# A quarter of a shared expert issued inside the stage before it, and a new plan of every engine's order

## The chip, the cores and the metric

The kernel runs on one core of one Trainium2 chip. The metric is the device time of one execution in microseconds; smaller is better. Of the kernel before there are three timed runs and one execution taken by the hardware profiler.

## The reference

The input is x, 2048 tokens of 128 channels, in float32. Four layers follow one another, each with a mixing part and a feed-forward part, and each part ends with `x = layernorm(x + part(x))` or the like. For this change two parts of the third layer matter, a chunked attention part and a mixture of experts with one shared expert that all tokens pass:

```
# L2 attention: 8 sequences of 256 tokens, each on its own
x = la attention, lf feed-forward, sa attention, pf feed-forward (each with its norm)
x = layernorm(x + ...)

# L2 experts ("moe2"): E=8, K=2, capacity 320 rows each
xn = xf * rsqrt(mean(xf*xf) + eps);   logits = xn @ router_w.T
topk_p, topk_i = top_k(softmax(logits), 2);  rw = topk_p / sum(topk_p)
dispatch = for each expert the first 320 tokens that chose it
eout = (silu(xg @ rg) * (xg @ ru)) @ rd            # per expert, 320 x 128, inner size 512
routed = eout, weighted, added back to the rows they came from
shared = silu(x @ sg) * (x @ su) @ sd              # all 2048 tokens, inner size 1024
x = layernorm(x + shared + routed)
```

After it comes the fourth layer: an attention with decay ("typed" here), again over 8 sequences of 256 tokens, and a ternary linear layer.

## The kernel before

The kernel runs six stages in a row: `rglru`, `local_mamba`, `moe1`, `chunked`, `moe2`, `typed`. Channels lie on the 128 partitions, tokens along the free axis, all in SBUF between stages.

**Who sets the order.** The Python code records instructions stage by stage. Then the class `_Order` takes all of them with their dependences and plans, engine by engine, in which order they are issued. It simulates the engines with a table of lengths per form of instruction (`LENGTHS`: busy time and latency in nanoseconds), ranks instructions by the place where the code recorded them plus a correction by engine, tile and stage (`BIAS`), and prefers to stay with what an engine is set to (`STAY`: a rank bonus for the same shape of TensorE tile, and for the same activation table on ACT). A table change is charged `TABLE` = 1283 ns. `impose` fixes the order found. So a change at one place, or a new number in these tables, moves instructions everywhere.

**Activation tables.** ACT must hold the table set of the function that it runs. Exp and Ln share one set (group 1 in `SETS`), Silu, Gelu and Sigmoid have their own. In the kernel before, the code itself places loads of the Exp/Ln set by hand (`exp_ln`, which calls `keep`), at places that the order then has to respect; one more hand-placed load fetches the Silu set early in the first routing (`if t0:`). All other loads are put in by the compiler just ahead of the activation that needs them.

**The chunked stage.** `on_pe` interleaves the eight sequences in three streams; `one_sequence(b)` goes through attention `la`, feed-forward `lf`, attention `sa`, feed-forward `pf`, a norm, `logits`, and `route2`. The stage's PSUM banks are K (3), A (2), B (1) and M (2). `route2` ranks two experts per token on VectorE (small instructions), with Exp/Ln on ACT for the row scale (`four`), counts ranks with a product on TensorE (`cum`), and scatters rows into the buffer `places` on POOL, four indirect DMAs (L1623) per sequence. Sequence 7 needs the counts of sequence 6 (`sum2`). By the time the last sequence runs out there are few streams left to fill TensorE; this is called the tail here.

**The moe2 stage** has banks A (2), B (2), M (3) and S (1). The shared expert is done in four quarters of 512 tokens, each a generator `shared(i)` with eight steps ("blocks"): `pg` and `pu` (128x512 products), Silu on ACT (L2052), a multiply on VectorE (L2057, tile `sh`) and four products into `acc`. Order in the code: two steps of `shared(0)`, the rest of the last routing, `rows_of` (five transfers `got<-places`, of which the second and fourth are issued on ACT's queue, L1643), the other steps of `shared(0)`, the eight experts (`bt` transposes, `pg`, `pu`, `py`, rows written to `ybuf`), then `shared(1)` to `shared(3)`, with 32 indirect gathers from `ybuf` on POOL (L1658) beside them: four at once, then one for each step, held by a wait for the Silu of that step:

```python
            for _ in shared(1):
                next(fetch)
            self.x = y
            first = chain(results(0, self.ty), self.typed_before(0))
            for i in (2, 3):
                for _ in shared(i):
                    next(first, None)
                    next(fetch, None)
```

`results` multiplies the gathered rows by their gates and normalises; `typed_before` prepares a sequence of the typed attention, with rotations `q`, `k` (L2205), masked keys `km` (L2212) on POOL. The typed stage's softmax multiplies `e` (L2262) are on POOL too.

Of the kernel before, what the change touches and what calls it, by code (L numbers as in the profile page):

```python
# [311 lines left out]
class _Order:  # L312
# [14 lines left out]
    STAY = dict(PE=80, ACT=740)  # L327
    BIAS = {
        "ACT  1": 100, "ACT  5": 585, "ACT bt 3": 5, "ACT bt 5": -775, "ACT d 2": -425, "ACT da 2": -45, "ACT e 2": -5, "ACT e 4": 965, "ACT e 6": -20,
        "ACT got 3": 575, "ACT h 2": -200, "ACT ix 4": 15, "ACT k 2": 265, "ACT lavp 2": 210, "ACT lnrs 1": -10, "ACT lnrs 2": -160, "ACT lnsq 1": -135,  # L330
        "ACT lnsq 2": 15, "ACT ot 2": 10, "ACT ptsb 2": -595, "ACT ptsb 6": -515, "ACT q 2": 20, "ACT qsq 2": 10, "ACT r 2": -5, "ACT rg 1": 10,
        "ACT rg 2": -915, "ACT rn 2": 15, "ACT rs 4": 340, "ACT rs 6": -690, "ACT s 6": 200, "ACT sakq 2": -10, "ACT sg 3": -550, "ACT sh 5": -2525,
        "ACT spe 1": -220, "ACT spt 1": -50, "ACT st 6": 100, "ACT sz 2": 280, "ACT v 2": 885, "ACT vs 4": 320, "ACT xchunked 2": 15, "ACT xs 2": -610,
        "DVE biasfull 3": -335, "DVE biaspart 3": -20, "DVE bt 5": -5, "DVE c 1": 590, "DVE centre 0": 320, "DVE d 2": 10, "DVE decaypart 4": -600,
        "DVE e 4": 570, "DVE four 4": 100, "DVE fs 4": -70, "DVE gate 4": 340, "DVE get 2": 200, "DVE got 4": 530, "DVE identb 0": -50, "DVE k 6": 500,
        "DVE lg 2": 2240, "DVE lo 4": -265, "DVE mv 4": -660, "DVE mv 5": 100, "DVE mv 6": -485, "DVE nm 2": -3975, "DVE nm 6": 4960, "DVE nth 4": -45,
        "DVE oh 2": -725, "DVE oh 5": -10, "DVE ptsb 2": -3895, "DVE ptsb 6": 895, "DVE put 4": -395, "DVE put 5": 55, "DVE q 5": -825, "DVE q 6": -475,
        "DVE rc 2": -1225, "DVE rc 6": 10, "DVE route 2": -55, "DVE s 5": 10, "DVE sares 2": 70, "DVE sel 2": -1590, "DVE sg 3": -140, "DVE sm 4": 2720,
        "DVE spl 1": -215, "DVE ss 2": 370, "DVE st 4": 85, "DVE st 6": 1645, "DVE sum 4": 170, "DVE t 2": 440, "DVE u 2": 250, "DVE vs 4": 50,
        "DVE we 4": 1425, "DVE xc 2": 460, "DVE xla 4": -15, "DVE xlocal 2": -5, "DVE xmoe 5": -200, "DVE xmoe 6": -580, "DVE xpf 4": -370,  # L340
        "DVE xrglru 2": 120, "DVE xsa 4": 80, "DVE z 4": -1990, "PE a 2": -100, "PE acc 5": 155, "PE b 2": -35, "PE bt 3": 75, "PE bt 5": 50,
        "PE cum 2": -995, "PE cum 4": -25, "PE cum 5": -615, "PE fold 2": 2915, "PE g 2": -4155, "PE gate 2": 785, "PE kps 4": 135, "PE less 2": 295,
        "PE lg 2": 1680, "PE lg 4": 50, "PE ln 2": -10, "PE o 2": 10, "PE o 6": -10, "PE pg 5": 150, "PE ps 4": -15, "PE pt 4": -130, "PE pu 3": 220,
        "PE py 3": -200, "PE py 5": 170, "PE qk 2": 25, "PE qkt 2": -720, "PE raw 2": -8675, "PE rows 2": 400, "PE sc 2": -50, "PE sc 4": 65, "PE sc 6": 5,
        "PE v 5": 290, "PE vps 2": 4075, "PE vps 4": 25, "PE wo 2": 75, "PE wo 6": -85, "PE wout 2": -115, "PE xin 2": 1180, "PE xps 2": -2540, "PE y 2": 20,
        "PE z 2": -450, "PE zt 5": 560, "PE zt 6": 25, "POOL d 2": 130, "POOL e 6": -30, "POOL got 4": -200, "POOL h 2": 370, "POOL k 5": 400,
        "POOL k 6": 850, "POOL km 6": 1240, "POOL mean 0": 1510, "POOL places 5": -200, "POOL q 6": 20, "POOL rest 4": -65, "POOL rg 1": -800,
        "POOL rg 2": -200, "POOL rot 2": -400, "POOL s 6": -750, "POOL t 2": 550, "POOL zero 0": -655, "POOL zeros 1": 385, "SP bc 2": -970, "SP cst 3": 5,
        "SP got 3": 355, "SP got 5": 350, "SP rottable 0": 80, "SP rows 4": 210, "SP rowschunked 4": -105, "SP vec 0": -830, "SP w 0": 15, "SP w 3": 115,
        "SP wattn 2": 585, "SP wffn 2": 705, "SP wlocal 0": 1175, "SP wmoe 4": 520, "SP xs 2": -105, "SP ybuf 5": -200,  # L350
    }
    LENGTHS = {
        "ACT  LoadActFuncSet  ": (1178, 1283), "ACT d Ln 128x512 128x512": (535, 640), "ACT da Exp 128x255 128x255": (398, 503),
        "ACT e Abs 128x256 128x256": (460, 565), "ACT e Exp 128x128 128x128": (420, 525), "ACT e Exp 128x256 128x256": (461, 566),
        "ACT e Exp 128x512 128x512": (527, 632), "ACT four Exp 128x2 128x2": (100, 205), "ACT got DMACopy 128x512 128x512": (454, 3611),
        "ACT h TensorCopy 64x255 64x255": (295, 400), "ACT lnrs Exp 128x256 128x256": (315, 420), "ACT ot TensorCopy 128x512 128x512": (486, 591),
        "ACT qsq Square 128x512 128x512": (494, 599), "ACT r Relu 128x256 128x256": (460, 565), "ACT rg Exp 128x1020 128x1020": (1039, 1144),
        "ACT rg Exp 128x1024 128x1024": (998, 1103), "ACT rg Ln 128x1024 128x1024": (950, 1055), "ACT rn Exp 128x16 128x16": (110, 215),
        "ACT rn Ln 128x16 128x16": (112, 217), "ACT rs Exp 128x2 128x2": (96, 201), "ACT rs Ln 128x2 128x2": (98, 203),
        "ACT sh Silu 128x512 128x512": (492, 597), "ACT v TensorCopy 128x512 128x512": (485, 590), "ACT xc Identity 128x256 128x256": (460, 565),  # L360
        "ACT xc Silu 128x512 128x512": (526, 631), "ACT xchunked TensorCopy 128x256 128x256": (263, 368), "ACT xmoe Identity 128x256 128x256": (404, 509),
        "ACT xs TensorCopy 33x256 33x256": (257, 362), "ACT xsq Square 128x128 128x128": (297, 402), "DVE biaspart TensorCopy 96x256 96x256": (197, 282),
        "DVE decay TensorScalarPtr 128x512 128x512": (508, 593), "DVE decaypart TensorCopy 128x512 128x512": (331, 416),
        "DVE four TensorScalarPtr 128x4 128x4": (76, 160), "DVE ge TensorScalarPtr 128x256 128x256": (380, 465),
        "DVE ge TensorScalarPtr 85x256 85x256": (372, 457), "DVE got TensorScalarPtr 128x128 128x128": (258, 343),
        "DVE h TensorTensor 128x256 128x256": (312, 397), "DVE hs TensorScalarPtr 128x1024 128x1024": (2189, 2274),
        "DVE hs TensorTensor 128x1024 128x1024": (1116, 1201), "DVE mv BNStatsAggregate 128x2 128x6": (82, 167),
        "DVE nm TensorTensor 128x8 128x8": (66, 151), "DVE ptsb TensorCopy 128x512 128x512": (589, 674), "DVE rc Reciprocal 128x16 128x16": (160, 245),
        "DVE rc Reciprocal 128x4 128x4": (84, 169), "DVE rc Reciprocal 128x8 128x8": (106, 191), "DVE rg TensorScalarPtr 128x256 128x256": (577, 662),
        "DVE rg TensorTensor 128x1024 128x1024": (1109, 1194), "DVE rottable TensorScalarPtr 128x256 128x256": (261, 346),  # L370
        "DVE s TensorScalarPtr 128x128 128x128": (247, 332), "DVE s TensorTensor 128x256 128x256": (323, 408),
        "DVE sm TensorReduce 128x16 128x512": (593, 678), "DVE ss TensorReduce 128x8 128x512": (594, 679), "DVE st BNStats 128x6 128x128": (197, 282),
        "DVE sum TensorReduce 128x32 128x448": (810, 895), "DVE t TensorScalarPtr 128x256 128x256": (384, 469),
        "DVE t TensorTensor 128x512 128x512": (593, 678), "DVE vec TensorTensor 128x1 128x1": (59, 144), "DVE vec TensorTensor 85x1 85x1": (59, 144),
        "DVE vs TensorCopy 128x512 128x512": (594, 679), "DVE wlocal TensorScalarPtr 128x682 128x682": (481, 566),
        "DVE x TensorScalarPtr 128x256 128x256": (368, 453), "DVE xc TensorScalarPtr 128x254 128x254": (383, 468),
        "DVE xc TensorScalarPtr 128x255 128x255": (384, 469), "DVE xla TensorScalarPtr 128x256 128x256": (442, 527),
        "DVE xlocal TensorTensor 128x256 128x256": (311, 396), "DVE xpf TensorScalarPtr 128x256 128x256": (562, 647),
# [64 lines left out]
    def group(self, i):  # L443
# [5 lines left out]
        if e == "ACT":  # L449
            return 1 if op == "LoadActFuncSet" else self.SETS.get(str(x.func).split(".")[-1]) if op == "Activation" else None  # L450
        return None

    def change(self, i):
        x, e, op = self.ops[i]
        if e == "ACT":
            return 0.0 if op == "LoadActFuncSet" else self.TABLE
# [315 lines left out]
class _Kernel:  # L772
# [125 lines left out]
    def exp_ln(self, last=None):  # L898

        i = self.nc.scalar.preload_act_table_set("natural_log_exp_and_others")  # L900
        if last is not None:
            self.issue_after([i], last)
# [1508 lines left out]
```

## Time and profile before

| | before |
|---|---|
| median of 3 runs | 1642.47 us (1641.91 to 1643.14) |
| profiled execution, own time | 1644.68 us |
| its span | 1642.9 us |
| mean granted TensorE clock | 0.942 |
| PE busy | 1417.4 us, 86% |
| DVE (VectorE) busy | 1102.3 us, 67% |
| ACT (ScalarE) busy | 968.6 us, 59% |
| POOL (GpSimd) busy | 587.5 us, 36% |

"PE" is TensorE's matmul, "PEld" its weight load. The profiled execution is 2.2 us longer than the median. A line of a timeline gives the start, the duration, the engine, the source line, the operation with output and inputs, the count, and in brackets how long the engine had been idle and what released it; "issue" means that nothing in the profile held it. A line of windows gives a stretch of the span, its length, the busy time and count of each engine, the granted clock (1.00 is full speed), the DMA share and GB/s. Shares over the whole span are averages over stages with different limits. By the tiles in the trace `rglru`, `local_mamba` and `moe1` take up to about 862 us, `chunked` with its tail up to about 1288 us, `moe2` up to about 1442 us, and `typed` the rest.

### The profile page before, as it was taken

How to read it: one execution, taken by the hardware profiler on the slowest of the kernel's cores; microseconds unless marked ns; L12 is line 12 of the kernel's file. 1: busy time of each engine (PE TensorE's matmuls, PEld its weight loads, DVE VectorE, ACT ScalarE, POOL GpSimd, SP SyncE). 2: the span in 40 equal slices, each digit the busy share in tenths (PEclk: the TensorE clock that was granted, in tenths of full speed). 3: DMA queues.
4: the chain of work that ended last, by engine and by line, in shares of the span. 5: the costliest groups of instructions: out<-in, count | busy, mean ns of one | idle time of the engine just before them, and what ended most of it. 6: DMA issues, size and time to landing. Idle time of an engine off the chain costs nothing. (4 is left out here: it accounts for less than half of the span.)

```text
span 1642.9 us, 28581 instructions
## 1 busy us (share of the span) xinstructions
PE 1417.4 (86%) x10826; PEld 909.4 (55%) x10826; DVE 1102.3 (67%) x2182; ACT 968.6 (59%) x2656; POOL 587.5 (36%) x535
## 2 busy tenths in 40 slices
PE   2688998989898887777579999999998899899997
PEld 1354554545554544334366766777675576556664
DVE  5745568898989898698545557554546333279886
ACT  3777888787978869446125545455453222167775
POOL 1334544535462523101431222212212102467774
PEclk7789999989999999779789999999998899999998
DMA  5000012121212223155430000000000130000000
GB/s 199 1 1 1 1 40 65 40 60 45 65 40 65 53 52 91 52 179 189 151 119 1 8 12 11 10 5 8 32 18 24 46 121 26 26 9 8 5 8 11
DMA packets 45113, 77.97 MB, mean 47 GB/s; under 512 B 5580, under 2 KB 21988, under 8 KB 43824
## 3 DMA queue, kind: packets, MB, share of 16 engines
q1 hardware_dynamic: 39648, 70.02, 14.0%
q0 software_dynamic: 3216, 5.07, 1.1%
q8 instruction: 85, 1.39, 0.4%
q10 hardware_dynamic: 2112, 1.05, 0.2%
q14 instruction: 52, 0.43, 0.1%
HBM read 66.87 MB, written 10.76 MB: 47 GB/s over the span
## 5 line engine op out<-in xcount | busy, mean ns | idle before, releaser
L870 PE MATMUL y<-hs,ident 128*128 128x512 f32 x256 | 139.7, 659 | 35.9 <-DVE hs L1307 35.6
L1158 POOL TENSOR_TENSOR e<-e,rc 128x1024 f32<-128x1024 f32 x32 | 78.0, 2437 | 202.7 <-DVE rc L1157 194.3
L1306 DVE TENSOR_TENSOR_SCAN hs<-da,hs 128x1024 f32<-128x1024 f32 x64 | 149.1, 2331 | 0.2
L2259 ACT ACTIVATE e<-sc,nm 128x128 f32<-128x128 f32 (+1 forms) x256 | 105.2, 427 | 46.6 <-DVE nm L2254 40.3
L1153 ACT ACTIVATE e<-sc,nm,rn 128x128 f32<-128x128 f32 x256 | 114.3, 466 | 13.8 <-DVE nm L1148 13.5
L981 PE MATMUL pt<-ident,e 128*128 128x128 f32 x768 | 114.2, 278 | 9.4 <-POOL e L1158 4.9
L1302 ACT ACTIVATE da<-d,na 128x255 f32<-128x255 f32 x256 | 109.3, 504 | 17.5 <-DVE hs L1306 13.7
L1836 POOL TENSOR_TENSOR e<-e,rc 128x512 f32<-128x512 f32 x32 | 34.0, 1064 | 219.8 <-DVE rc L1835 154.2
L981 PEld LDWEIGHTS pt<-ident,e 128*128 128x128 f32 x768 | 88.5, 141 | 42.5 <-issue 16.1
L2262 POOL TENSOR_TENSOR e<-e,rc 128x1024 f32<-128x1024 f32 x48 | 90.8, 1896 | 39.1 <-DVE rc L2261 32.1
L1105 POOL TENSOR_TENSOR t<-t,t 128x512 f32<-128x512 f32 x64 | 83.9, 1316 | 58.0 <-DVE t L1092 51.6
L1811 ACT COPY kp<-kps 128x512 f32<-128x512 f32 x128 | 74.7, 583 | 49.0 <-PE kps L870 46.4
L1658 POOL DMA_INDIRECT got<-ybuf,get x48 | 45.7, 952 | 159.2 <-DMA ybuf<-ys 97.1
L870 PEld LDWEIGHTS y<-hs,ident 128*128 128x128 f32 x256 | 48.5, 205 | 82.5 <-DVE hs L1307 54.2
L1304 DVE TENSOR_TENSOR hs<-u,bc 128x1024 f32<-128x1024 f32 x64 | 84.3, 1328 | 2.9 <-POOL u L1291 2.9
L1307 DVE TENSOR_TENSOR hs<-hs,bc 128x1024 f32<-128x1024 f32 x64 | 80.6, 1260 | 0.0
L1847 ACT COPY vs<-vps 128x512 f32<-128x512 f32 x64 | 37.4, 585 | 67.1 <-PE vps L870 53.6
L983 DVE COPY ptsb<-pt 128x512 f32<-128x512 f32 x104 | 68.8, 675 | 11.6 <-PE pt L981 9.3
L870 PE MATMUL qk<-w_local,h 128*128 128x512 f32 x128 | 69.3, 631 | 7.5 <-DVE t L1092 7.1
L870 PE MATMUL vps<-sa_vp,x_lf 128*32 128x512 f32 x512 | 68.4, 594 | 0.0
L1847 DVE COPY vs<-vps 128x512 f32<-128x512 f32 x64 | 43.3, 682 | 37.2 <-PE vps L870 25.1
L2057 DVE TENSOR_TENSOR sh<-sh,pu 128x512 f32<-128x512 f32 x32 | 22.0, 688 | 67.1 <-PE pu L870 54.0
(380 smaller groups left out, 3782.4 us busy)
## 6 DMA issues: line engine op xcount, KB each, us to landing
bc<-xs SPq DMA_DIRECT2D x128, 256.0 KB
w_moe<-in_e_dram SPq DMA_DIRECT2D x16, 768.0 KB
w_attn<-in_w_dram SPq DMA_DIRECT2D x4, 1024.0 KB
w_local<-in_w_dram SPq DMA_DIRECT2D x2, 1557.0 KB
places<-zeros SPq DMA_DIRECT2D x2, 1280.0 KB
got<-places SPq DMA_DIRECT2D x6, 256.0 KB
ybuf<-ys SPq DMA_DIRECT2D x8, 160.0 KB
x_in<-in_x_dram SPq DMA_DIRECT2D x1, 1024.0 KB
```

The source lines that it names most:

```text
L870: return self.nc.tensor.matmul(out, lhsT, rhs, start=start, stop=stop)
L981: self.last = self.nc.tensor.transpose(pt[:, j * P : (j + 1) * P], src[:, j * P : (j + 1) * P], self.ident)
L1105: nc.gpsimd.tensor_add(t1, t1, t2)
L1153: nc.scalar.activation(e[:, j, g, :], scs[:, j, g, :], AF.Exp, bias=nm[:, j, g : g + 1], scale=rq[:, j, g : g + 1], accum_out=sm[:, j, g : ...
L1158: nc.gpsimd.tensor_tensor(e, e, rc.unsqueeze(3).to_broadcast([P, 2, 4, P]), ALU.mult)
L1302: nc.scalar.activation(da[:, n, c, 1:S], d[:, c, 1:S], AF.Exp, scale=na[:, i : i + 1])
L1304: nc.vector.tensor_tensor(hs, u.unsqueeze(1).to_broadcast(shp), bn, ALU.mult)
L1306: nc.vector.tensor_tensor_scan(line(hs), line(da), line(hs), 0.0, ALU.mult, ALU.add)
L1307: nc.vector.tensor_tensor(hs, hs, cn, ALU.mult)
L1847: i = copy(v[:, c, :, :].rearrange("p a b -> p (a b)"), ps)
L2259: nc.scalar.activation(e[:, i, :], sc[:, i, :], AF.Exp, bias=nm[:, i : i + 1], accum_out=sm[:, i : i + 1])
L2262: nc.gpsimd.tensor_tensor(e, e, rc.unsqueeze(2).to_broadcast([P, n, keys]), ALU.mult)
```

## The change

1. The first quarter of the shared expert, `shared(0)`, is taken out of `moe2` and issued within the last sequence (`b == B - 1`) of `chunked`, a step at a time between the steps of its last feed-forward, norm and output. Its `pg` and `pu` go to bank K, its `acc` to bank M; its tile has a ring of four (tag "e"). Its result `s0` is a slice of the tile of the shared expert's second weight, which is 1536 columns wide instead of 1024.
2. In `moe2`, `shared(1)` now stands where `shared(0)` stood, around the last routing and the dispatch. Behind the experts only `shared(2)` and `shared(3)` are left, with two gathers for each step instead of one; the results of the first typed sequence are advanced only beside `shared(3)`.
3. All hand-placed table loads go (`exp_ln`, `keep`, the early Silu load). `impose` puts in a load of the Exp/Ln set, once the order is planned, wherever an Exp or Ln follows another set. The planner no longer sees loads as instructions of their own; it charges `TABLE` for each change of set.
4. `STAY`, `BIAS` and `LENGTHS` have new values, so the planned order of every engine differs in all stages. The numbers of instructions are the same on every engine but for table loads on ACT: 69 before, 74 after. Ahead of the tail there were 65 and are 58; in the tail and `moe2` there were 4 and are 16 (eight of the Silu set and eight of Exp/Ln, 13 of these up to the first Silu of `shared(1)`).

The diff, without the tables of numbers and places where only an `exp_ln` line goes:

```diff
-    STAY = dict(PE=80, ACT=740)
+    STAY = dict(PE=90, ACT=980)
     BIAS = {
...
     def impose(self):
         order, _ = self.plan()
+        ring, last = [], None
+        for i in order["ACT"]:
+            g = self.groups[i]
+            if g is not None:
+                if g == 1 != last:
+                    load = self.tc.nc.scalar.preload_act_table_set("natural_log_exp_and_others")
+                    self.ops.append((load.ins, "ACT", "LoadActFuncSet"))
+                    ring.append(len(self.ops) - 1)
+                last = g
+            ring.append(i)
+        order["ACT"] = ring
...
-        i = nc.scalar.activation(lg, lg, AF.Exp)
-        if t0:
-
-            j = nc.scalar.preload_act_table_set("silu_and_others")
-            self.issue_after([j], i)
-            self.keep(j)
+        nc.scalar.activation(lg, lg, AF.Exp)
...
+                early = iter(())
                 if b == B - 1:
                     self.weights_shared()
+                    self.norm = None
+                    early = self.shared(0, y, self.s0, work, ("K", "M"), tag="e", bufs=4)
...
+                next(early, None)
                 z = yield from self.ffn(x3, w[:, 1, :], "pf", add, work, small)
+                next(early, None)
+                next(early, None)
 
                 zt = self.by_channel(z)
...
+                next(early, None)
                 yield 0.3, 0.6
                 out = self.psum("M", "out").rearrange("p (t d) -> p t d", t=4)
...
                 z = self.normed(out[:, 0:2, :], work, small, "z")
+                next(early, None)
+                next(early, None)
                 yield 0.3, 2.5
...
                 nc.scalar.copy(y[:, cs], self.by_channel(z))
+                for _ in early:
+                    pass
                 yield 0.3, 0.8
...
-        down = self.fw.tile([P, 1024], F32, tag="la_vp", name="w_shared")
+        down = self.fw.tile([P, 1536], F32, tag="la_vp", name="w_shared")
+        down, s0 = down[:, 0:1024], down[:, 1024:]
+        self.s0 = s0.rearrange("p (t d) -> p t d", t=4)
...
+    def shared(self, i, x, s, work, banks=("A", "S"), tag="sh", bufs=None):
...
+            yield
+        s = s.rearrange("p t d -> p (t d)")
+        nc.vector.tensor_add(s, acc, s)
...
-            common = shared(0)
+            common = shared(1)
...
-            for _ in shared(1):
-                next(fetch)
             self.x = y
             first = chain(results(0, self.ty), self.typed_before(0))
             for i in (2, 3):
                 for _ in shared(i):
-                    next(first, None)
+                    next(fetch, None)
+                    if i == 3:
+                        next(first, None)
                     next(fetch, None)
```

The body of the new `shared` is that of the old inner function: `pg`, `pu`, Silu, multiply, four `acc` products, then the add of the rows, with the banks, the tile's tag and its ring as arguments.

## The prediction

> **What bounds the kernel now.** I read the page's shares first (PE busy 86% of 1642.9 us, DVE 67%, ACT 59%, POOL 36%), then busy time by window, to find where PE, the bound, is not full. Columns: window, its length, busy time of PE, PEld, DVE, ACT, POOL, granted clock, DMA share, GB/s.
>
> ```profile
> 655.00:862.00 207.00, 142.43 (x733) 91.06 (x734) 140.82 (x206) 84.09 (x177) 48.24 (x42) 0.83 0.42 137
> 1250.00:1258.00 8.00, 7.51 (x48) 5.86 (x47) 7.13 (x42) 4.15 (x12) 3.07 (x5) 1.00 0.01 2
> 1258.00:1288.00 30.00, 18.34 (x70) 10.89 (x69) 15.77 (x92) 7.84 (x29) 13.24 (x14) 0.72 0.27 73
> 1288.00:1385.00 97.00, 97.00 (x502) 68.49 (x501) 31.16 (x65) 24.47 (x50) 2.77 (x3) 1.00 0.21 63
> 1385.00:1442.00 57.00, 48.10 (x208) 30.98 (x207) 18.93 (x42) 12.78 (x20) 31.32 (x33) 0.91 0.11 32
> ```
>
> PE is full through the experts (97 of 97). It loses 0.5 + 11.7 = 12.2 us in the tail of the chunked stage, and 8.9 after the experts. The PE timeline of the tail shows the waits, and a second loss:
>
> ```profile
> 1269.89 2.06 PE L870 MATMUL pg<-x_chunked,w_shared 128*128 128x512 f32 x2
> 1277.29 2.08 PE L870 MATMUL pg<-x_chunked,w_shared 128*128 128x512 f32 x2 [3.58 <-ACT sh L2052]
> 1284.15 1.12 PE L870 MATMUL pg<-x_chunked,w_shared 128*128 128x512 f32 x2 [1.70 <-ACT sh L2052]
> 1286.87 1.02 PE L870 MATMUL pg<-x_chunked,w_shared 128*128 128x512 f32 x2
> ```
>
> The same product takes 2.06 us at half clock and 1.02 at full: four such pairs lose 1.0 each and one acc group 0.7, about 5 us. ACT's timeline says why PE waited: a table load, then a queue held by a DMA issue that waits for the scatters.
>
> ```profile
> 1275.35 1.28 ACT L2052 ACT_TABLE_LOAD   x1
> 1276.64 0.60 ACT L2052 ACTIVATE sh<-pg 128x512 f32<-128x512 f32 x1
> 1282.44 1.02 ACTq L1643 DMA_DIRECT2D got<-places  x2
> 1283.50 0.60 ACT L2052 ACTIVATE sh<-pg 128x512 f32<-128x512 f32 x1 [6.26 <-issue]
> ```
>
> After the experts one ACT wait costs PE most of its loss; the releaser "remote" names no cause.
>
> ```profile
> 1402.79 0.60 ACT L2052 ACTIVATE sh<-pg 128x512 f32<-128x512 f32 x1 [11.52 <-remote]
> 1403.44 2.07 PE L870 MATMUL pg<-x_chunked,w_shared 128*128 128x512 f32 x2 [6.07 <-ACT sh L2052]
> ```
>
> Last, POOL, which owns the 32 gathers:
>
> ```profile
> 1381.62 0.99 POOL L1658 DMA_INDIRECT got<-ybuf,get  x1 [97.06 <-DMA ybuf<-ys]
> 1382.92 0.97 POOL L1658 DMA_INDIRECT got<-ybuf,get  x1 [0.31 <-issue]
> 1406.42 0.95 POOL L1658 DMA_INDIRECT got<-ybuf,get  x1 [1.80 <-ACT sh L2052]
> 1416.62 0.73 POOL L2205 TENSOR_TENSOR k<-k,t 128x256 f32<-128x256 f32 x1
> 1417.43 3.75 POOL L2212 TENSOR_TENSOR km<-k,cst 128x1024 f32<-128x1024 f32 x2
> 1449.34 1.90 POOL L2262 TENSOR_TENSOR e<-e,rc 128x1024 f32<-128x1024 f32 x1
> ```
>
> Free, a gather takes 1.25 us; paced by a shared block it takes 2.61. So gathers have slack now.
>
> **The boundary, term by term.** From the end of the second attention (1249.74) to the first expert product (1300.79) is 51.05 us. In it are eight shared blocks of 2.61 (pg 0.86, pu 0.86, acc 0.89 apart), 20.9; idle 12.2; half clock 5.0; so the tail's own products need about 13.0. In the changed kernel quarter 0 and quarter 1 both lie there, and eight blocks (20.9) go from behind the experts. PE then needs: own 13.0; quarter 0 20.9; a rest of waits up to the last routing product (cum); quarter 1 20.9; and what the dispatch still exposes.
>
> Rest of waits up to cum: zero if the blocks cover all, 6.9 if none (12.2 less the 5.3 above that belong to the ACT queue). I followed the planned order: most z and rs waits (2.75 + 2.06 on DVE) now have blocks beside them, but ACT has much more: its own work in the two windows is 4.15 + 7.84 less a load and four Silus, 8.3; eight Silus 4.8; 13 table loads (Silu and Exp/Ln alternate in the planned order) of 1.28, 16.7. That is 29.8 us against 37 of PE work, so it is not the bound in sum; but a load stands ahead of small Exp/Ln links of the routing chain. Some Silu loads carry the wait for pg themselves; queued behind one on ACT are the Exp/Ln of rs and four, for which DVE's z and PE's transposes wait. And acc holds one of the two M banks, so out and zt of both last sequences share the other. I take 3.2.
>
> The transfers moved with quarter 0 cost nothing: the shared weights are issued at 1183.7 and 1192.7 and were first used at 1269.9, so a use some 15 us earlier leaves over 60 us; the rows of quarter 0 are four sequences old, and are added only after its last block. Without that cover a late weight would stop the blocks, and rival 1 would start sooner.
>
> Dispatch: from cum (1273.45) to the first bt transpose (1288.59) is 15.1 us: four scatters, the got DMA, its landing. Six blocks of quarter 1 left then are 15.7, a cover of 0.6 only. The ACT queue still has the two got issues between its first Silus, so I carry the old waits, 3.58 + 1.70 = 5.3 (zero if Silus get ahead of them, 8 if they come later), and half clock on one block after, 2.07 + 1.92 + 1.65 against 1.02 + 1.02 + 1.05, 2.5 us.
>
> Sum 13.0 + 20.9 + 3.2 + 20.9 + 5.3 + 2.5 = 65.8, against 51.05 + 20.9 = 71.95: **-6.2 us** (-16 at best, -1 if all bounds are bad).
>
> The Trainium skill speaks against this: "ScalarE: Activation LUTs", section "Table sets: the hidden batching unit", says to batch activations by table set, and "What ACT_TABLE_LOAD costs" adds a drain of about 1.38 us to each load. Here the load at 1275.35 ends at 1276.63 and the Silu starts at 1276.64, so I see no drain after it. By the page ACT would have 47.7 us in the tail, 11 more than PE, and the gain would be gone.
>
> **After the experts.** Sixteen blocks instead of 24 cover the gathers. POOL needs 32 x 1.25 + q 0.74, k 0.73, km 3.75 = 45.2 us from the landing of ybuf, about 12.5 us after the first block of quarter 2 (call it S). Eighteen gathers stand ahead of q: to S + 35.7; km ends S + 44, and the first score product is due S + 48. The eleven gathers left take 13.7 more and stand ahead of the first softmax multiply (L2262): POOL free at S + 58 where that multiply could end at S + 57.5, so it ends 4 us late: **+4** (0 to +10, as the order on POOL puts gathers or multiplies first).
>
> The 11.52 us wait: PE's 6.07 idle and 2.5 of half clock hang on it, and the trace gives no cause. Other orders may or may not hit it; I take 0.4 of 8.6: **-3.4** (0 to -8.6).
>
> **Table loads elsewhere.** All loads go from 69 to 74, but those ahead of the tail from 65 to 58: 7 x 1.28 = 9.0 us of ACT. Four are in the first 64 us, where PE is busy only 9.7 of the first 40; there ACT is in the chain. I take **-2** (0 to -5.1). The Silu load of the first experts, hidden before at 804.36, now sits behind the wait for its product: **+0.6** (0 to 1.3).
>
> **The new plan.** Biases and lengths are all new, so each engine's order changes in all stages; the work is equal. The stretch most open to this is 655 to 862, with 64.6 us of PE idle. Nothing in the trace gives a sign: 0, with +-8 for the range.
>
> **Sum.** -6.2 + 4 - 3.4 - 2 + 0.6 = -7.0 against the profiled execution's 1644.68, so 1637.7. That execution is 2.2 over the median of 1642.47: **1635.5**.
>
> **Rivals.** (1) *ACT's loads delay the routing chain: slower.* It decides when cum comes later than PE has blocks: each microsecond over 37 to 38 after the attention is lost at full price, for dispatch has just 0.6 of cover. If half the 16.7 us of loads falls between links of that chain, 8.3 more, plus 2.5 of half clock: 1635.5 + 10.8 = 1646.3. For: loads that wait for a product block the queue, as the got issue does at 1282. Against: ACT has 7 us to spare. Chance 0.17. (2) *The new plan loses in the earlier stages*: 8 us, 1643.5 to 1647. For: 64.6 us idle whose order matters; against: fewer loads. 0.13. (3) *Gathers bind the typed start*, +10 instead of +4: 1641.5; the 45.2 us of POOL work have about 45 to fit in. 0.08. (4) *More than I count*: the got issues hold no Silu (-7.8) and the remote wait goes (-5.2): 1622.5. For: the idle windows are that large. 0.14. That the change does nothing in place, quarter 0 issued behind the routing, is excluded by the planned PE order, which has its blocks among ffn and norm products. My forecast has 0.48.
>
> **How the numbers follow.** About 0.2% (3.3 us) is what a measurement here tells from no change. The forecast, with a spread of some 6 us, lies faster in 0.40 of 0.48 and the same in 0.06; rival 4 is all faster; 3 is the same for the most part; 1 and 2 are slower in 0.22 of 0.30 and the same in 0.06. Faster 0.56, same 0.18, slower 0.26. The range leaves out the ends of rivals 4, 1 and 2: 1621 to 1649; faster cases alone would be 1621 to 1639.
>
> **What would show it.** Right: PE idle from the attention's end to the first expert product falls from 12.2 to 5 to 9 us, that stretch is 63 to 66 us long, a Silu waits "issue" for 4 to 6 us at the got DMAs, and gathers run 1.25 apart into the first scores. Wrong: cum later than 40 us after the attention; a gap of over 0.1 us behind each table load; more PE idle in 655 to 862 than 64.6; or no gather beside the first scores.

## The result, and the profile after

The changed kernel takes 1668.63 us (median of 4 runs, 1668.40 to 1670.64) against 1642.19 us of the kernel before beside it (4 runs, 1638.17 to 1643.14): a ratio of 1.0165, with a 95% interval of 1.0145 to 1.0186. It is 26 us slower, where 7 us faster was forecast. Its profiled execution has a span of 1666.8 us, 23.9 more than before.

I cut both spans, one profiled execution of each kernel, at the same products on PE. Times in us; "first expert" is the start of the first `pg<-bt` of `moe2`, "score" the start of the first `sc<-km` of the typed stage.

| stretch | before | after | difference |
|---|---|---|---|
| start to first scan product (y) | 261.9 | 264.6 | +2.7 |
| to last scan product | 531.2 | 538.2 | +7.0 |
| to first chunked score product (first experts) | 65.0 | 67.8 | +2.8 |
| to end of second attention | 391.7 | 395.2 | +3.4 |
| to first expert | 51.0 | 62.2 | +11.2 |
| to last shared product | 140.3 | 121.6 | -18.7 |
| to first typed score | 1.0 | 5.4 | +4.4 |
| to the end | 200.8 | 211.9 | +11.1 |

The boundary did what was forecast: quarter 0 costs 20.9 us of products, and the stretch grew by only 11.2. The losses are elsewhere. The windows of the changed kernel (columns as in the prediction) over the tail, the experts and the 5.4 us ahead of the typed scores:

```profile
655.00:862.00 207.00, 142.04 (x674) 88.40 (x673) 142.88 (x199) 83.13 (x185) 39.84 (x38) 0.80 0.44 139
1265.72:1327.90 62.18, 56.45 (x273) 36.62 (x274) 32.33 (x147) 35.01 (x65) 16.48 (x18) 0.97 0.16 42
1327.90:1449.50 121.60, 109.17 (x550) 75.88 (x548) 39.02 (x90) 28.97 (x55) 30.81 (x32) 0.96 0.19 58
1449.50:1454.92 5.42, 0.49 (x2) 0.33 (x3) 0.95 (x3) 0.00 (x0) 4.20 (x5) 0.79 0.19 53
```

PE's idle time in the tail fell from 12.2 to 5.7 us. In 655 to 862 PE is as busy as before, but this window now ends earlier in the work. PE's timeline, for the waits:

```profile
1305.88 2.07 PE L877 MATMUL pg<-x_chunked,w_shared 128*128 128x512 f32 x2 [2.73 <-ACT sh L2034]
1311.44 1.13 PE L877 MATMUL pg<-x_chunked,w_shared 128*128 128x512 f32 x2 [1.03 <-ACT sh L2034]
1425.43 2.07 PE L877 MATMUL pg<-x_chunked,w_shared 128*128 128x512 f32 x2 [9.79 <-ACT sh L2034]
1454.92 2.08 PE L877 MATMUL sc<-km,q 64*128 64x512 f32 x4 [4.82 <-DVE s L2045]
```

The first two are the dispatch behind the got issues. The third is the old wait of ACT beside the gathers, longer than before (9.79 against 6.07 us on PE); the fourth is new. ACT's timeline for the loads in the tail, the got issue and that wait; DVE's for the new one:

```profile
1282.51 1.28 ACT L763 ACT_TABLE_LOAD   x1
1283.81 0.30 ACT L1771 ACTIVATE rs<-mv 128x2 f32<-128x2 f32 x2
1309.69 1.05 ACTq L1628 DMA_DIRECT2D got<-places  x2
1310.79 0.60 ACT L2034 ACTIVATE sh<-pg 128x512 f32<-128x512 f32 x1 [4.96 <-PE acc L877]
1424.78 0.60 ACT L2034 ACTIVATE sh<-pg 128x512 f32<-128x512 f32 x1 [12.07 <-remote]
1454.09 0.69 DVE L2045 TENSOR_TENSOR s<-acc,s 128x512 f32<-128x512 f32 x1 [4.33 <-remote]
```

The Exp/Ln behind the load starts 0.02 us after the load's end: the load costs its 1.28 us and no more. The Silu behind the got issue starts 0.05 us after the end of that issue; its own product pg ended about 1307.9, so the issue held it for the last 3 of the 4.96 us, whatever the profile names as releaser. POOL's timeline, with the gathers 1.25 us apart into the first scores:

```profile
1400.02 0.98 POOL L1643 DMA_INDIRECT got<-ybuf,get  x1 [88.21 <-DMA ybuf<-ys]
1421.31 0.94 POOL L1643 DMA_INDIRECT got<-ybuf,get  x1 [0.30 <-issue]
1454.48 0.95 POOL L1643 DMA_INDIRECT got<-ybuf,get  x1 [0.30 <-issue]
```

One thing is needed to read the experiments: they ran in five groups, each beside its own runs of the kernel before, which took about 1630 us in the first and third group and 1644 in the others; the kernels profiled in those two groups lack the waits called "remote" and, with the order of before, some 8 us of the chunked stage (the kernel before has no profile there).

### The profile page after: what moved, and what is told of

Its sections match the earlier page's. It is cut to its first block, busy times and chain, and to the rows that moved or that the text cites. A ratio compares the mean times of both kernels' runs of the same rounds, so it can differ in the third digit from the quotient of the medians.

```text
span 1666.8 us, 28603 instructions
## 1 busy us (share of the span) xinstructions
PE 1440.4 (86%) x10826; PEld 917.5 (55%) x10826; DVE 1099.8 (66%) x2182; ACT 973.8 (58%) x2661; POOL 573.6 (34%) x535
## 3 DMA queue, kind: packets, MB, share of 16 engines
q10 hardware_dynamic: 2112, 1.05, 0.2%
## 5 line engine op out<-in xcount | busy, mean ns | idle before, releaser
L1150 POOL TENSOR_TENSOR e<-e,rc 128x1024 f32<-128x1024 f32 x32 | 72.3, 2259 | 224.5 <-DVE rc L1149 217.3
L974 PE MATMUL pt<-ident,e 128*128 128x128 f32 x768 | 118.3, 281 | 11.6 <-ACT ptsb L976 5.7
L2258 POOL TENSOR_TENSOR e<-e,rc 128x1024 f32<-128x1024 f32 x48 | 90.7, 1896 | 53.0 <-DVE rc L2257 51.2
L976 DVE COPY ptsb<-pt 128x512 f32<-128x512 f32 x104 | 68.9, 675 | 12.1 <-PE pt L974 11.5
L877 PE MATMUL sc<-msk,identb 128*128 128x512 bf16 (+2 forms) x224 | 53.5, 378 | 20.2 <-ACT e L1145 20.2
L877 PE MATMUL vps<-sa_vp,x_lf 128*32 128x512 f32 x512 | 67.8, 595 | 0.0
L2250 DVE TENSOR_REDUCE nm<-sc 128x4 f32<-128x1024 f32 (+1 forms) x48 | 58.4, 1217 | 13.9 <-PE sc L877 13.8
```

Of the source, the lines that this page charges most:

```text
L877: return self.nc.tensor.matmul(out, lhsT, rhs, start=start, stop=stop)
L974: self.last = self.nc.tensor.transpose(pt[:, j * P : (j + 1) * P], src[:, j * P : (j + 1) * P], self.ident)
L1150: nc.gpsimd.tensor_tensor(e, e, rc.unsqueeze(3).to_broadcast([P, 2, 4, P]), ALU.mult)
L2258: nc.gpsimd.tensor_tensor(e, e, rc.unsqueeze(2).to_broadcast([P, n, keys]), ALU.mult)
```

## The experiments

**What of the change costs: numbers, loads or structure (first group).** Four kernels, each with one part changed back or made alone.

e1, the changed kernel with the old numbers:

```diff
-    STAY = dict(PE=90, ACT=980)
+    STAY = dict(PE=80, ACT=740)
     BIAS = {
-        "ACT d 2": -105, "ACT da 2": -10, "ACT got 3": 450,
+        "ACT  1": 100, "ACT  5": 585, "ACT bt 3": 5,
...
     LENGTHS = {
...
```

> The changed kernel with STAY, BIAS and LENGTHS of the kernel before: quarter 0 in the tail, two gathers a block and the automatic table loads stay, the plan's numbers are undone. Theory (the moved quarter gains, the new numbers lose): stretch from the end of the second attention to the first expert product 60 to 64 us, typed period 23.2 us a sequence instead of 24.5, end of the second attention near 1250 instead of 1266; time 1634 to 1643. Rival (the moved quarter or the automatic loads cost it): typed period or the start of the experts stays late, time 1655 to 1670.

e2, the kernel before with the new numbers (the reverse edit):

> The kernel before with STAY, BIAS and LENGTHS of the changed one, nothing else. Theory: the loss comes with the numbers, so the end of the second attention is at 1262 to 1268, the typed period 24.3 to 24.7 us, and the time, without the gain at the boundary, 1662 to 1680. Rival (structure or loads cost it): 1638 to 1648.

e3, the kernel before, its numbers kept, with the planned loads in place of the hand-placed ones:

```diff
+                if g == 1 != last:
+                    load = self.tc.nc.scalar.preload_act_table_set("natural_log_exp_and_others")
...
-        self.exp_ln(last)
```

> The kernel before with its own numbers, but hand-placed table loads gone and the planned ones put in. Theory: nearly nothing, 1638 to 1646; the first score product of the local attention comes some us earlier. Rival (loads that sit in front of their activation stall ACT in all stages): 1650 to 1665.

e4, the changed kernel with the old `BIAS` of PE alone:

```diff
-        "PE a 2": -670, "PE acc 4": 555, "PE b 2": 790,
+        "PE a 2": -100, "PE acc 5": 155, "PE b 2": -35,
...
```

> The changed kernel with the BIAS entries of PE alone taken from the kernel before; all others, STAY and LENGTHS stay new. Theory (TensorE's own order is what got worse: products that can run side by side on parts of the array are split by others): typed period 23.2 to 23.5 us, PE busy in sum below 1420 us, time 1634 to 1648. Rival (the orders of ACT, DVE and POOL, or the new lengths, cost it): 1655 to 1670 with PE busy near 1440.

Measured, with the stretches of the table above (e9 is told below; up to the tail TensorE's order in it is that of before):

| | e9 | e1 | e2 | e3 | e4 |
|---|---|---|---|---|---|
| median, us | 1623.05 | 1671.78 | 1663.18 | 1659.07 | 1646.55 |
| ratio to before | 0.996 | 1.0242 | 1.0203 | 1.0174 | 1.0089 |
| 95% interval | 0.9944 to 0.9977 | 1.0212 to 1.0272 | 1.0173 to 1.0234 | 1.0144 to 1.0205 | 1.0056 to 1.0121 |
| scans | 528.9 | 556.8 | 553.2 | 551.8 | 532.7 |
| table loads in the scans | 40 | 46 | 46 | 46 | 43 |
| chunked to end of second attention | 383.2 | 384.1 | 378.9 | 385.3 | 386.7 |
| to first expert | 62.5 | 70.3 | 54.4 | 51.0 | 70.1 |
| to last shared product | 111.4 | 111.1 | 130.1 | 131.7 | 114.3 |
| to first typed score | 1.0 | 14.3 | 1.0 | 1.0 | 1.0 |
| first score to the end | 203.7 | 202.8 | 210.2 | 200.9 | 209.9 |

My theory was that the new numbers lose and the rest gains. It fell for the scans: the planned loads under the old numbers (e3) lose 21 to 23 us there (against 531.2 before and 528.9 in e9), and so do the new numbers under hand-placed loads (e2), 22 to 24 us; together they lose 7 or less (538.2 after, against 531.2). So numbers and way of loading fit each other, and a plan made with one of them alone is worse there. In the three kernels with long scans ACT has six more table loads there, 46 against 40, 7.7 us of ACT; that is a part of it, and how the rest comes about is not shown. By their times, e1 and e3 landed at their rivals (e1 just above, e3 within); e2 came out as its theory said (1663.18 us, end of the second attention at 1264.5), but as a sum of longer scans and a shorter chunked stage.

In the chunked stage itself the new numbers gain here: 378.9 us in e2 against 383 to 385 in e9, e1 and e3. For the typed stage the theory held: 210 us in the kernels of this table with the new numbers, 201 to 204 with the old ones. e4 shows that PE's biases alone do not make it. Its median of 1646.55 us lies in the range of its theory, but that range was set for a kernel before of 1642 us, and beside 1630 it is a loss of 0.9%; its typed stage stays at 209.9.

**The same two kernels again, the quarter undone, the pairs mended (second group).** e5 and e6 are the kernel before and the changed one, unedited. e7 is the changed kernel with `shared(0)` back in `moe2`, one gather a block, new numbers and planned loads. e8 adds this to the changed kernel, after the plan:

```diff
+            if self.stage[pe[k]] == 6 and self.key[pe[k]] == "PE sc" and self.groups[pe[k]][0] == 64:
+                for j in range(k + 1, min(k + 8, len(pe))):
+                    y = self.ops[pe[j]][0]
+                    if self.key[pe[j]] == "PE sc" and self.groups[pe[j]][0] == 64 and y.outs[0].bass_ap.tensor.name == x.outs[0].bass_ap.tensor.name:
+                        pe.insert(k + 1, pe.pop(j))
+                        break
```

> The kernel before once more, unchanged, for a profile on the chip of the runs beside it. If the 11.5 us wait of ACT after the experts belongs to the kernel, it is there again; if it comes from the chip or its state, it is gone and the stretch from the first expert product to the last shared product is near 131 us instead of 140.

> The changed kernel once more, unchanged, beside the kernel before on this chip. Same loss in the plan: typed period 24.5 us, scans 7 us longer; without the waits of ACT and DVE at the gathers, if this chip has none, 10 to 15 us less than 1668: 1645 to 1668, still slower than before by 15 to 25 us.

> The changed kernel with only quarter 0 put back into the experts' stage and the gathers one a block, as before; the new numbers and the automatic loads stay. Theory (the quarter in the tail gains 6 to 10 us as forecast): 6 to 10 us slower than the changed kernel, with the typed period still 24.5. Rival (the quarter costs more than it gains, through the later dispatch and the packed gathers): as fast as the changed kernel or faster.

> The changed kernel with one more step after the plan: where another product stands between the two score products of one typed unit (each on one half of the array's rows), the second is put right behind the first. Five of 48 pairs are split in the changed kernel, none in the kernel before. Theory (a split pair runs one after the other, about 1.1 us each): typed period 23.3 to 23.6 us, 5 to 6 us faster than the changed kernel. Rival (the typed loop is bound elsewhere): no change.

Against 1644.82 us of the kernel before: e6 1666.83 us, ratio 1.0131 (1.0103 to 1.0158), so the loss repeats; e7 1660.93, 1.0111 (1.0079 to 1.0143); e8 1661.54, 1.0099 (1.0071 to 1.0127). The kernel before has its wait of ACT again, 11.60 us. e7 is not slower than e6, so its theory fell and its rival held: from the end of the second attention to the first score both take 191 to 192 us (e7 54.3 + 137.0 + 1.0, e6 63.0 + 122.9 + 5.4). What the quarter gains ahead of the experts goes again behind them.

e8 settles a piece of the typed stage. In the kernel before the two score products of a unit, each on 64 rows of the array, stand side by side; in the changed kernel a product of v is between them in one unit of a sequence. PE's timelines, before, then after:

```profile
1544.33 1.13 PE L870 MATMUL sc<-km,q 64*128 64x512 f32 x4
1545.30 0.38 PE L870 MATMUL sc<-decay,onesb 64*128 64x512 bf16 x2
```

```profile
1567.43 1.12 PE L877 MATMUL sc<-km,q 64*128 64x512 f32 x2
1568.48 0.49 PE L877 MATMUL v<-w,x_moe 128*128 128x128 f32 x2
1568.90 1.12 PE L877 MATMUL sc<-km,q 64*128 64x512 f32 x2
1569.95 0.28 PE L877 MATMUL sc<-msk,identb 128*128 128x256 bf16 x1
```

Both products together take 0.97 us, start to start; each of the split ones takes 1.05. The period, from one typed sequence to the next in the steady part of the stage, is as long as these windows of the kernel before, the changed one and e4. PE is full in the first two, so a wait view shows nothing of the loss:

```profile
1530.98:1554.22 23.24, 23.12 (x218) 14.16 (x214) 20.42 (x53) 16.65 (x77) 17.05 (x11) 1.00 0.03 8
```

```profile
1551.27:1575.81 24.54, 24.54 (x217) 14.44 (x216) 20.50 (x53) 16.59 (x77) 17.14 (x11) 1.00 0.02 7
```

```profile
1554.52:1578.44 23.92, 23.18 (x219) 14.37 (x215) 20.91 (x53) 16.62 (x79) 17.13 (x12) 1.00 0.02 6
```

Over the typed sequences the group of these products (count, then busy time in us) shows it, in the changed kernel and in e8:

```profile
L877 PE MATMUL sc<-km,q 64*128 64x512 f32 x152 | 48.5, 641 | 0.0
```

```profile
L888 PE MATMUL sc<-km,q 64*128 64x512 f32 x152 | 42.9, 641 | 0.0
```

With the pairs kept, the typed period goes from 24.54 to 23.93 us (23.24 before). So a split pair costs 0.6 us net, about half of what I expected, and five of them 3 us of the 11. The whole typed stage is 3.9 us shorter in e8 than in e6; the medians differ by 5.3, more than the pairs explain. Which products make the other 0.7 of the period was not tried one by one, but e4 narrows it down: with PE's old biases all pairs but one stand together and PE is busy 23.18 us a period, as before. There the period is still 23.92, because PE now waits 0.7 us a sequence for VectorE (tile `ptsb`), whose order is still the new one.

**The quarter alone, and the order of the gathers (third group).** e9 is the kernel before with its numbers and hand-placed loads; only the quarter is moved, two gathers go with each block, planned loads are added where an Exp follows a Silu in the tail, and five new `BIAS` entries come along. e10 leaves these five out. e11 is the changed kernel with half the gathers.

```diff
+        "PE acc 4": 555, "PE pg 4": 490, "PE pu 4": 1925, "DVE sh 4": -40, "POOL got 5": 3790,
```

```diff
-                        got[k].append(self.gather(keep, ybuf, self.get2[:, k], t, f"got{k}{t}"))
+                        got[k].append(got[0][t] if k else self.gather(keep, ybuf, self.get2[:, k], t, f"got{k}{t}"))
```

> The kernel before with its own numbers and hand-placed loads, so that TensorE's order is that of before up to the tail; only quarter 0 is moved into the tail, with two gathers a block after the experts and planned table loads where an Exp follows a Silu there. Five BIAS entries of the changed kernel for the moved tiles (pg, pu, acc, sh in the chunked stage, got in the experts') come with it. Theory (the move itself is good, the new numbers lose): end of the second attention and typed period as before (23.2 us), tail to first expert product 62 to 66 us, ratio to before 0.992 to 0.998. Rival (what the boundary gains goes again after the experts, to the gathers): ratio 0.999 to 1.004.

> The same without the five BIAS entries: 26 of the 32 gathers then stand ahead of the first typed q on POOL, instead of 10. Theory (gathers bind the typed start when packed in front): first typed score product 8 to 14 us later after the last shared product than in the run beside it, time 6 to 12 us longer. Rival (POOL has slack): same time.

> The changed kernel with 16 gathers instead of 32: the rows of the second expert choice are not fetched, the first ones are used in their place (that part of the computation is left out). Theory (the waits of ACT and DVE after the experts that the profile calls remote belong to the unbroken train of gathers): train of 8 to 10 gathers, wait below 5 us or gone, first expert product to last shared product 109 to 115 us instead of 122. Rival (they belong to the place in the program): a wait of 11 us or more stays.

Against 1629.67 us: e9 1623.05, ratio 0.996 (0.9944 to 0.9977), the only variant that does the whole work and is faster than the kernel before; e10 1641.74, 1.0074 (1.0045 to 1.0103); e11, which leaves out half of the gathers, one run of 1621.48. The windows of e9 from the end of the second attention to the first score:

```profile
1238.34:1300.84 62.50, 56.39 (x277) 37.33 (x278) 33.33 (x148) 34.52 (x65) 16.47 (x18) 0.97 0.16 42
1300.84:1412.22 111.38, 108.99 (x548) 76.57 (x546) 39.12 (x90) 28.96 (x55) 24.36 (x25) 0.98 0.20 59
1412.22:1413.22 1.00, 0.02 (x3) 0.05 (x2) 1.00 (x5) 0.00 (x0) 0.85 (x1) 1.00 0.26 74
```

That is 174.9 us against 183.7 in e3 (51.0 + 131.7 + 1.0), which has no moved quarter and ran without the waits too: the move is worth about 9 us where nothing takes it back. The typed stage of e9 takes back 2.8 of them (203.7 against 200.9). e10 shows the price of the gathers in front, on POOL and then on PE:

```profile
1433.30 0.94 POOL L1824 DMA_INDIRECT got<-ybuf,get  x1 [0.30 <-issue]
1436.30 7.45 POOL L2391 TENSOR_TENSOR km<-k,cst 128x1024 f32<-128x1024 f32 x4
```

```profile
1438.24 2.08 PE L1036 MATMUL sc<-km,q 64*128 64x512 f32 x4 [0.76 <-POOL km L2391]
```

The 32 gathers end at 1434.2, the masked keys come after them, and the first score is 14.3 us behind the last shared product instead of 1.0, as in e1, which lacks the five entries too. Without them its tail also loses 7.7 us to the first expert (70.2 against 62.5).

**The waits called remote (fourth and fifth group).** e12, e17 and e15 are the changed kernel (twice) and the kernel before, unedited; e13 is e9 and e14 is e11 again. e16 is e9 with the gathers spread into the typed stage:

```diff
-                            self.wait_for(self.gathered, self.silu)
+                            self.wait_for(self.gathered, self.paced if self.late else self.silu)
...
+                while self.late and len(got[1]) < min(2 * b + 4, NT):
+                    next(fetch, None)
```

> The changed kernel unchanged, once more, since chips differ: on the chips of the first and of the second pair of changed and old kernel ACT and DVE wait 4 to 13 us beside the gathers and the chunked stage takes 391 us in the kernel before, on two others there is no such wait and it takes 384. Theory (these waits and the chunked stage are what the new plan loses more of on such a chip): without the waits 1618 to 1632 and within 0.5% of before, with them 1660 to 1670. Rival (the loss is in the order alone, the same on all chips): 1.0 to 1.7% slower than before here too.

> The quarter alone, with the old numbers and the hand-placed loads, beside the changed kernel. Where the waits are there: the train of gathers is in two parts of 10 and 15, so 3 to 9 us of waits, ratio to before 0.996 to 1.003. Where they are not: 0.994 to 0.998 as in its first run. In both cases faster than the changed kernel where the old numbers are the better ones (theory), or not (rival).

> The changed kernel with 16 gathers (the second choice's rows are not fetched), beside the changed kernel itself. Theory (the waits come with the length of the train): the waits named remote shrink to less than 5 us; the stretch from the first expert product to the first typed score product is 8 to 18 us shorter than in the changed kernel where that has the waits, 0 to 2 where it has not. Rival: same waits.

> The kernel before, for a profile on this chip: chunked stage 383 to 385 us and no wait of ACT beside the gathers, or 391 and the wait of 11.5; the two go together if one property of the chip makes both.

> The quarter alone (old numbers, hand-placed loads), with the gathers spread: five at once and one a block beside quarter 3, 13 in all, and the other 19 within the typed stage, three or four a sequence, each held until a reciprocal of the softmax two units back. No train is longer than 7. Theory (the waits come with long trains, and the boundary gain is real): no wait above 3 us on ACT or DVE after the experts, first typed score product 1 us after the last shared product, ratio to before 0.983 to 0.991 where the kernel before has its 11.5 us wait, 0.990 to 0.997 where it has not. Rival (gathers inside the typed loop cost POOL what they free before): ratio 0.998 or more.

> The changed kernel unchanged beside it. With the waits as in its first, second and third run: 1.3 to 1.6% slower than before. Without them: within 0.6% of before, since only the numbers' loss in the scans (5 us) and in the typed loop (10 us) stays, against 9 us of the boundary and 6 of the chunked stage.

Against 1644.28 us: e12 1669.32, ratio 1.0141 (1.0115 to 1.0168); e13 1644.55, 1.000 (0.9983 to 1.0017); e14 1645.05, 1.0005 (0.9988 to 1.0021); e15 one run of 1643.57, with ACT's wait (11.77) and the chunked stage at 392.2. Against 1644.26: e16 1653.02, 1.0052 (1.0034 to 1.0070); e17 1670.21, 1.0158 (1.0136 to 1.0180). Both last groups had the waits, so the changed kernel was never run whole without them. e12 was to tell whether its loss goes with the waits or with the order alone; with the waits there, its 1.4% fits both.

With half the gathers ACT's wait falls from 12.81 (e12) to 5.27 us and DVE's 4.37 is gone; from first expert to first score e14 takes 112.0 us, e12 126.9. (Less than 5 us of wait and 8 to 18 us of gain were expected.) ACT's wait in e14, and the last gather of its train:

```profile
1409.84 0.60 ACT L2034 ACTIVATE sh<-pg 128x512 f32<-128x512 f32 x1 [5.27 <-remote]
```

```profile
1407.78 0.94 POOL L1643 DMA_INDIRECT got<-ybuf,get  x1 [0.31 <-issue]
```

The wait ends 1.1 us after that gather. In e13 the same waits come back in another place: DVE waits 7.43 us and the first score comes 12.6 us after the last shared product, instead of 1.0 in e9, so the gain is gone. e16 was meant to avoid them with trains of three to six, and lost: each train of four within the typed stage stops ACT and then PE.

```profile
1517.21 0.37 ACT L1133 COPY s<-zt 128x256 f32<-128x256 f32 x1 [2.78 <-remote]
```

```profile
1517.64 0.69 PE L1132 MATMUL zt<-ident,s 128*128 128x128 f32 x2 [2.11 <-ACT s L1133]
```

Its typed period is 27.28 us instead of 23.24; the first score did come 1.0 us after the last shared product, as expected.

## Why the prediction was wrong

**The boundary held.** Forecast -6.2, measured 62.2 - 71.95 = -9.8. The stretch was 62.2 us (63 to 66 were named), the wait of a Silu at the got issues 4.96 us (4 to 6, though only some 3 of it are the issue's), the idle time of PE 5.7 us (5 to 9; the sum had 3.2 + 5.3). The last cum came 35.4 us after the attention, so rival 1 did not happen. Thirteen table loads in the tail cost 1.28 us each and did not lengthen the stretch beyond the forecast. The drain of about 1.38 us that the Trainium skill adds to each load ("ScalarE: Activation LUTs", "What ACT_TABLE_LOAD costs") is not in this trace: at eleven of the thirteen loads ACT is idle for 0.02 us or less behind the load, and at eleven for 0.02 us ahead of it. The 11 us by which ACT would then have outlasted PE were not lost.

**The term that failed is "the new plan: 0, with +-8".** I gave it no sign and small bounds, and looked for it in PE's idle time in 655 to 862. In this pair of profiles it is +2.7 ahead of the scans (forecast -2), +7.0 in the scans, +2.8 in the first experts (forecast +0.6), +3.4 in the chunked stage and about +11 in the typed stage: 27 us together. Rival 2 had the mechanism in the earlier stages, at half of what they lost here (8 of 16 us); neither it nor I had the typed stage, where PE is full and so no idle time warned of it. e1 to e3 show how large such a term can get: the plan's numbers go with one way of loading, and 552 to 557 us in the scans is what a plan gets when they do not match. The claim "the work is equal" was true in instructions and false in time, as a product split from its pair shows.

Two parts of the term behave differently. Up to the end of the second attention, profiles of one and the same order of PE differ by 6 to 14 us. In the groups with the waits, seven with the changed kernel's order reach that end at 1254.5 to 1268.9 us, mean 1262.5, and five with the order of before at 1246.6 to 1252.8, mean 1250.0; so 12.5 us is a better figure than 16. In the groups without the waits the difference is gone: e11, which has the changed kernel's order there, comes to 1240.0, e9 and e10 to 1238.3 and 1242.7. The chunked stage alone takes 378.8 us in e11, less than the 383.2 of e9; with the waits the changed kernel's order needs 393.5 to 395.7. Why the new order loses there only in the groups with the waits is not shown. The typed stage loses in both: 9 us in e2 against e3, 9 in e7 (209.9) against the kernel before; the 2 us left go with the moved quarter and its packed gathers, which e7 does not have.

What the changed kernel would take without the waits is an estimate: e11's 1621.48, plus 2.9 us from first expert to first score (112.4 in e9, 109.5 in e11) and 3.4 in the typed stage (211.9 in e12, 208.4 in e14) for the gathers that e11 leaves out, about 1628 against 1629.67 of the kernel before. That would be level, not 7 us faster; it rests on one run.

The signs named ahead could not catch this. Those for "right" came true or nearly so in a kernel that is 26 us slower, since they watch the boundary alone; the one for the plan, more PE idle than 64.6 us in 655 to 862, came out at 64.96 over a window that ends earlier in the work, and says nothing.

**The front.** The first score product of the local attention came 7.5 us earlier (63.9 against 71.4), as fewer loads promised. By the first scan product it was 2.7 us later: in that stretch the mask products wait 15.0 us for ACT's Exp, before 4.6. The gain was real, and given back within the same stage; how much more than that is open, for this stretch varies from 258.8 to 264.9 us among profiles of the changed kernel's order.

**The wait of 11.52 us.** I counted on 0.4 of it going, -3.4. It stayed, grew (12.07), and a second one came on DVE (4.33): the first expert to the last shared product lost 2.2 beside the removed 20.9, and the first score another 4.4. The step that failed was to take it for an accident of the order. Within the groups that have the waits, ACT's goes with the gathers' train, which this change made longer: 5.3 us with 9 gathers without a break (e14), 5.9 with 13 (e7), 11.5 with 15 (before), 12.1 with 18 (after).

**The gathers.** +4 was forecast at the first softmax multiply through POOL's queue. Its own figures give less: POOL free at S + 58 and a multiply of 1.90 us, against an end at S + 57.5, is 2.4. The typed start did lose 4.4 us ahead of the first score, but by the wait of DVE. Behind it the queue costs about 2: the first softmax multiply starts 11.2 us after the first score, 9.1 in e7, where the gathers come one a block. Where the planner puts the gathers in front, as in e1 and e10, the queue itself costs 13 us; what keeps them back in the changed kernel is among the five `BIAS` entries, most likely that of got, which was not tried alone.

## What to carry to other kernels

When a change comes with a new plan, price the plan as the main term: cut both orders at the same instructions and look where small products that run side by side are separated, even where the engine shows no idle time. Change a planner's numbers, its structure and its table loads together or not at all, and try the structure alone under the old numbers first; here that, with five entries for the moved tiles, was the only whole variant that won (0.996), and only while the waits beside the gathers were absent (1.000 with them); without the five entries it lost (1.0074). Profile the same kernel more than once before you read a few microseconds of a long stretch. Work moved into idle time gains what the next stage can use of it: ask which stream, here the gathers, lost its cover.

## What the runs showed of the hardware

In the groups with the waits, a train of indirect gathers 1.25 us apart on POOL goes with a stop of ACT, DVE or PE that the profile calls "remote" or "issue", of 2 to 14 us. ACT's mostly ends 1.0 to 2.9 us after the end of the train's last gather (e16 1.0, e14 1.1, e12 1.2, the kernel before 2.6 to 2.9); DVE's 4.33 us in the changed kernel ended just ahead of it, and one of 5.3 us on ACT in e17 in the middle of the train, so the rule is not exact. In the kernel before, gathers 2.61 us apart show none. In the first and third group the same trains, up to 32 us long in e1 and e10, show none at all, and the chunked stage of the same plan is shorter: 383.2 us in e9 against 391.4 in e13, the same kernel on the same chip, and 378.8 in e11 against 395.2 in e14. The kernels of the third and fourth group ran on one chip, so it is not the chip alone; what differs was not found.
